# Moving two small VectorE operations: a lower limit to GpSimd, an affine step of the scan's decay to ScalarE

## The chip, the cores and the metric

The kernel runs on one core of a Trainium2 chip. Such a core has four engines that matter here: TensorE (PE in the profile; its weight loads are a row of their own, PEld), VectorE (DVE), ScalarE (ACT) and GpSimd (POOL). SyncE (SP) issues most of the transfers. Each engine takes its instructions in the order in which they stand in its own queue, and waits on semaphores for what other engines or transfers have to deliver. The metric is the device time of the whole kernel in microseconds (us). Before the change the median of three runs is 3594.73 us (3590.82 to 3597.36).

## The reference

The input x has 32 sequences of 256 tokens with 256 features. Two blocks follow each other, and x is added to their result.

```python
# block 1: a gated scan (d_inner 512, 16 states)
xr, gate = split(x @ W_in.T); xr = xr + t_emb
xc = silu(causal_conv4(xr) + b_conv)
xn = layernorm(xc) * ln_g + ln_b
Bm, Cm, dt = split(xn @ W_xproj.T, 3)
dt = tanh(dt @ W_dt.T + b_dt) * 0.01
Ad = 1.0 + dt * (-tanh(A_log))          # the decay factors
Bd = Bm * minimum(norm(xn), 1.0)
h  = clip(h * Ad + Bd * xt, -10, 10)    # 256 steps in order
y  = Cm . h + D * xn
out = (y * silu(gate)) @ W_out.T
# block 2, two layers (8 heads of 64, windows of 128 tokens)
q, k, v = split(shift(x) @ wqkv, 3)
q = q / clip(norm(q), 1e-12) * q_scale  # the same for k
q, k = rotary_xpos(q, k)
x = x + local_attention(q, k, v) @ wo
a, g = split(layernorm(shift(x)) @ w1 + b1)
x = x + (a * gelu(g)) @ w2 + b2
```

Two places matter: the decay factors `Ad`, and the lower limit that keeps the division of q and k by their lengths finite.

## The kernel before, in words

The 32 sequences are worked through in four groups of eight. The scan of a group runs in 8 chunks of 32 steps. All 128 lanes hold 16 states of 8 sequences; a step (line 716) is one VectorE instruction on a 128x512 tile that adds a row to the state and limits it. The kernel does not multiply the state by its decay. It carries the state divided by the running product `p` of the decays. For each chunk, `figures_in` (lines 627 to 639) makes the small tiles `bcd` and `beta`; `decay_th` (641 to 644) takes the hyperbolic tangent on ScalarE into `ad`, 128x32; `decays` (646 to 662) turns `ad` into decay factors on VectorE (648), multiplies them up with a scan instruction (650), takes the reciprocal (653), and from these makes `beta`, `ct` and the limits `lim`, the last on GpSimd (660, 661). Every step's row comes by a transfer from DRAM that repeats it over 16 states (`xrep`, 685, six buffers) and is scaled by its `beta` on ScalarE (706). TensorE reads the states out (728).

Block 2 works on one sequence at a time. `project_qkv` (984) multiplies for q, k and v and for two windows of 128 tokens. `rotated` (998 to 1023) handles one 128x512 tile of q or k, four per sequence and layer, 256 in all. ScalarE squares the tile (1002). VectorE makes the two rotary products (1005 and twice 1010) and sums the squares per head into `ss`, 128x8 (1015). VectorE then puts a lower limit on `ss` (1019). GpSimd adds the rotary products (1013), raises `ss` to the power -0.5 (1021) and scales the tile (1022). `turn` transposes the tile on TensorE (1028), and scores (1215), exponentials (1227), row sums (1252), their reciprocal on VectorE (1260), values (1271), output projection (1039) and the feed-forward part (1375 with gelu at 1386 and product at 1393, 1402) follow.

The order is set in two steps. The kernel's own code emits the work by slots: the scan's work hangs on step numbers, block 2's on eight slots per sequence, and the two are woven together, so that block 2 of one group runs beside the scan of the next. The framework's planner then orders the instructions of all engines by its own cost estimates, except where a line asks to keep the program's order. So a change of one instruction can move others in the queues. A chunk of the scan falls on two passes of a sequence through a layer. The first group's scan has nothing of block 2 beside it, and block 2 of the last group has no scan beside it.

All PSUM tiles come from one pool of eight banks. TensorE therefore also waits for VectorE or ScalarE to have read an older bank, whatever it was used for. The tiles `sq`, `swp` and the store tile `fo` share three buffers.

Of the kernel before, what the change touches and what calls it, by code (L numbers as in the profile page):

```python
# [13 lines left out]
AF = mybir.ActivationFunctionType  # L14
ALU = mybir.AluOpType
# [37 lines left out]
def bc(ap, axis, n):  # L53

    ap = ap.unsqueeze(axis)
    shape = list(ap.shape)
    shape[axis] = n
    return ap.broadcast_to(shape)
# [15 lines left out]
def kernel(  # L74
# [29 lines left out]
    nc = tc.nc  # L104
# [10 lines left out]
    def per_state(src, name):  # L115

        t = const.tile([P, 1], FP, tag=name, name=name)
        src = bc(bc(src, 1, GB), 2, 1)
        nc.scalar.dma_start(out=t, in_=src)
        return t  # L120
# [22 lines left out]
    a_sb = per_state(a_log, "a_sb")  # L143
# [24 lines left out]
    one = const.tile([P, 1], FP, tag="one", name="one")  # L168
# [53 lines left out]
    def program(ctx, exact):  # L222
# [154 lines left out]
        def group_scan(g):  # L377
# [263 lines left out]
            def decay_th(c):  # L641
                ad = sm.tile([P, CH], FP, tag="ad", name="ad")
                nc.scalar.activation(ad, ck[c]["bcd"][:, 2], AF.Tanh, bias=wbias[:, 2:3])
                ck[c]["ad"] = ad

            def decays(c):
                ad, bcd, beta = ck[c].pop("ad"), ck[c].pop("bcd"), ck[c]["beta"]
                nc.vector.tensor_scalar(ad, ad, a_sb, 1.0, ALU.mult, ALU.add)
                pd = sm.tile([P, CH], FP, tag="pd", name="pd")
                nc.vector.tensor_tensor_scan(pd, ad, zero_ch, state["p"], ALU.mult, ALU.add)  # L650
                state["p"] = pd[:, CH - 1 : CH]
                pi = sm.tile([P, CH], FP, tag="pi", name="pi")
                nc.vector.reciprocal(pi, pd)
                nc.vector.tensor_mul(beta, beta, pi)
                ct = sm.tile([P, CH], FP, tag="ct", name="ct")
                nc.vector.scalar_tensor_tensor(
                    ct, bcd[:, 1], wbias[:, 1:2], pd, ALU.add, ALU.mult
                )
                lim = sm.tile([P, 2, CH], FP, tag="lim", name="lim")
                nc.gpsimd.tensor_scalar_mul(lim[:, 0], pi, CLIP)  # L660
                nc.gpsimd.tensor_scalar_mul(lim[:, 1], pi, -CLIP)
                ck[c].update(ct=ct, lim=lim)
# [193 lines left out]
            for c in range(NCH):  # L856
# [28 lines left out]
                at(s0 - 9, figures, c)  # L885
                at(s0 - 7, figures_in, c)
                at(s0 - 6, decay_th, c)
                at(s0 - 5, decays, c)
                at(s0 - 4, put_c, c, 0)
                at(s0 + 4, put_c, c, 1)  # L890
# [107 lines left out]
        def rotated(l, ps, w, a):  # L998


            sq = ap_.tile([P, DI], FP, tag="swp", name="sq", bufs=3)
            nc.scalar.activation(sq, ps, AF.Square)  # L1002
            rot = ap_.tile([P, HEADS, DH], FP, tag="rot", name="rot", bufs=4)
            ph = ps.rearrange("p (h d) -> p h d", h=HEADS)
            nc.vector.tensor_mul(rot, ph, bc(rc_sb[:, l, w, a], 1, HEADS))  # L1005
            swp = ap_.tile([P, HEADS, DH], FP, tag="swp", name="swp", bufs=3)
            hd = DH // 2
            for i in range(2):
                o, s = slice(i * hd, (i + 1) * hd), slice((1 - i) * hd, (2 - i) * hd)
                nc.vector.tensor_mul(  # L1010
                    swp[:, :, o], ph[:, :, s], bc(rs_sb[:, l, w, a, o], 1, HEADS)
                )
            nc.gpsimd.tensor_add(rot, rot, swp)  # L1013
            ss = aw.tile([P, HEADS], FP, tag="ss", name="ss")
            nc.vector.tensor_reduce(
                ss, sq.rearrange("p (h d) -> p h d", h=HEADS), AX.X, ALU.add
            )

            nc.vector.tensor_scalar_max(ss, ss, 1e-24)  # L1019
            rn = aw.tile([P, HEADS], FP, tag="rn", name="rn")  # L1020
            nc.gpsimd.tensor_tensor(rn, ss, neg_half, ALU.pow)  # L1021
            nc.gpsimd.tensor_mul(rot, rot, bc(rn, 2, DH))  # L1022
            return rot
# [38 lines left out]
        def attention(l):  # L1062

            for b in range(GB):

                qTs, kTs, vs = [], [], []
                for w in range(NW):
                    for a in (2, 0, 1):
                        ps = project_qkv(b, w, a)
                        if a == 2:  # L1070
                            v_sb = ap_.tile([P, DI], FP, tag="v1", name="v_sb", bufs=3)
                            nc.scalar.copy(v_sb, ps)
                            vs.append(v_sb)
                            continue
                        rot = rotated(l, ps, w, a)
                        dst = ap_.tile(
                            [P, HEADS // 2, W], FP, tag="kT1" if a else "qT1",
                            name="kT" if a else "qT", bufs=3 if a else 2,
                        )
                        turn(rot, dst)  # L1080
                        (kTs if a else qTs).append(dst)
                        yield
# [71 lines left out]
        class Attention:  # L1154
# [9 lines left out]
            def project(self, b, w, a):  # L1164
                if w == 0 and a == 2:
                    self.qkv[b] = [
                        ap_.tile([P, HEADS // 2, S], FP, tag=n, name=n, bufs=1)
                        for n in ("qT", "kT")
                    ] + [ap_.tile([P, NW, DI], FP, tag="v", name="v_sb")]
                ps = project_qkv(b, w, a)  # L1170
                if a == 2:
                    nc.scalar.copy(self.qkv[b][2][:, w], ps)
                else:
                    self.rot[b, w, a] = rotated(self.l, ps, w, a)
# [487 lines left out]
```

## Time and profile before

| | |
|---|---|
| median of three runs | 3594.73 us |
| profiled execution, its own time | 3592.27 us |
| span of that profile, first to last instruction | 3590.5 us |
| TensorE busy | 3448.4 us, 96% |
| VectorE busy | 2667.8 us, 74% |
| ScalarE busy | 1979.5 us, 55% |
| GpSimd busy | 1874.5 us, 52% |
| line 1019, VectorE, x256 | 118.2 us, 462 ns each |
| line 648, VectorE, x32 | 22.0 us, 689 ns each |
| line 643, ScalarE, x32 | 10.2 us, 319 ns each |
| line 1021, GpSimd, x256 | 466.3 us, 1822 ns each |

A row of groups gives line, engine, operation, tiles and shapes, the number of instructions, their busy time and the mean of one, and then the idle time of the engine ahead of them with what ended it. Busy TensorE time is modelled from the instruction's size, so a stretch in which it is always busy is read together with the pitch of its instructions. The span falls into stages: up to about 475 us the first group's scan alone, to about 2700 us both blocks side by side, and then block 2 of the last group alone.

### The profile page before, as it was taken

How to read it: one execution, taken by the hardware profiler on the slowest of the kernel's cores; microseconds unless marked ns; L12 is line 12 of the kernel's file. 1: busy time of each engine (PE TensorE's matmuls, PEld its weight loads, DVE VectorE, ACT ScalarE, POOL GpSimd, SP SyncE). 2: the span in 40 equal slices, each digit the busy share in tenths (PEclk: the TensorE clock that was granted, in tenths of full speed). 3: DMA queues.
4: the chain of work that ended last, by engine and by line, in shares of the span. 5: the costliest groups of instructions: out<-in, count | busy, mean ns of one | idle time of the engine just before them, and what ended most of it. 6: DMA issues, size and time to landing. Idle time of an engine off the chain costs nothing.

```text
span 3590.5 us, 57544 instructions
## 1 busy us (share of the span) xinstructions
PE 3448.4 (96%) x20220; PEld 2253.8 (63%) x20220; DVE 2667.8 (74%) x5049; ACT 1979.5 (55%) x3535; POOL 1874.5 (52%) x1842
## 2 busy tenths in 40 slices
PE   7999989999999999999999999999999999999999
PEld 4545335566656666666666666666666677777777
DVE  5888989878788877877787888777777555555553
ACT  4656656656555655566566555665656444434442
POOL 4433467546556556655555566555545454544551
PEclk9999999999999999999999999999999999999999
DMA  7788755444444555444454555534353112011111
GB/s 201 215 209 220 201 156 151 131 112 139 129 134 127 147 146 142 138 117 125 118 140 127 135 149 139 146 107 130 113 143 118 56 49 64 13 30 36 34 27 37
DMA packets 468766, 435.67 MB, mean 121 GB/s; under 512 B 228723, under 2 KB 308084, under 8 KB 468340
## 3 DMA queue, kind: packets, MB, share of 16 engines
q1 hardware_dynamic: 384018, 419.88, 41.9%
q10 hardware_dynamic: 84450, 12.01, 2.0%
q8 instruction: 163, 2.67, 0.3%
q14 instruction: 135, 1.11, 0.1%
HBM read 383.54 MB, written 46.66 MB: 120 GB/s over the span
## 4 chain that ended last, share of the span: by engine, by line
PE 62%; DVE 19%; DMA 7%; POOL 5%; issue 3%; ACT 3%; SPq 1%; ACTq 0%; DVEq 0%; POOLq 0%
PE pa L1375 13%; PE ps_qkv L989 13%; DVE h L716 7%; PE po_f L1402 7%; PE ps_wo L1039 5%; DMA xrep<-xnd 5%; PE y L728 4%; PE ov L1271 3%; PE sc L1215 3%; PE ps_out L808 2%; PE ps_in L399 2%; PE tr_qk L1028 2%; PE rs L1252 2%; DVE acc L489 2%; PE ps_raw L518 1%
## 5 line engine op out<-in xcount | busy, mean ns | idle before, releaser
L716 DVE CUSTOM_DVE_ANT_0 h<-h,xrep,lim 128x512 f32<-128x512 f32 x1024 | 956.3, 934 | 195.5 <-ACT xrep L706 164.6
L706 ACT ACTIVATE xrep<-xrep,beta 128x512 f32<-128x512 f32 x960 | 673.6, 719 | 358.8 <-DMA xrep<-xnd 258.4
L989 PE MATMUL ps_qkv<-qkv,res 128*128 128x512 f32 x1536 | 713.5, 600 | 18.9 <-DVE rinv L1260 8.2
L1375 PE MATMUL pa<-hT,w 128*128 128x256 f32 (+1 forms) x2816 | 675.1, 382 | 11.8 <-DVE zT L799 11.4
L1375 PEld LDWEIGHTS pa<-hT,w 128*128 128x128 f32 (+1 forms) x2816 | 516.8, 188 | 153.6 <-issue 35.0
L1013 POOL TENSOR_TENSOR rot<-rot,swp 128x512 f32<-128x512 f32 x256 | 341.5, 1334 | 448.9 <-DVE swp L1010 399.5
L1021 POOL TENSOR_TENSOR rn<-ss,neg_half 128x8 f32<-128x8 f32 x256 | 466.3, 1822 | 16.7 <-DVE ss L1019 7.0
L989 PEld LDWEIGHTS ps_qkv<-qkv,res 128*128 128x128 f32 x1536 | 281.8, 191 | 302.3 <-issue 239.6
L728 PE MATMUL y<-h,ly 128*32 128x512 f32 x2048 | 347.2, 611 | 14.9 <-DVE h L716 13.9
L1327 POOL TENSOR_TENSOR rstd<-ve,neg_half 128x2 f32<-128x2 f32 x64 | 46.6, 727 | 524.6 <-DVE ve L1325 508.4
L1402 PE MATMUL po_f<-ag,w 128*128 128x256 f32 x1280 | 307.4, 387 | 6.9 <-DVE fo L1413 4.0
L1022 POOL TENSOR_TENSOR rot<-rot,rn 128x512 f32<-128x512 f32 x256 | 287.4, 1123 | 19.9
L1393 DVE SCALAR_TENSOR_TENSOR ag<-pa,b_sb,ag 128x256 f32<-128x256 f32 x320 | 151.6, 474 | 181.2 <-ACT ag L1386 181.0
L1402 PEld LDWEIGHTS po_f<-ag,w 128*128 128x128 f32 x1280 | 235.9, 191 | 72.0 <-issue 12.0
L1386 ACT ACTIVATE ag<-pa,b_sb 128x256 f32<-128x256 f32 x320 | 150.4, 470 | 232.6 <-PE pa L1375 231.5
L1002 ACT ACTIVATE sq<-ps_qkv 128x512 f32<-128x512 f32 x256 | 151.5, 596 | 199.8 <-PE ps_qkv L989 132.4
L489 DVE SCALAR_TENSOR_TENSOR acc<-xr,wc_sb,acc 128x256 f32<-128x256 f32 x384 | 196.9, 536 | 51.0 <-POOL acc L478 50.5
L1005 DVE TENSOR_TENSOR rot<-ps_qkv,rc_sb 128x512 f32<-128x512 f32 x256 | 174.9, 683 | 78.1 <-ACT sq L1002 77.7
L1039 PE MATMUL ps_wo<-oT,wo 128*128 128x256 f32 x1024 | 231.6, 379 | 0.0
L1039 PEld LDWEIGHTS ps_wo<-oT,wo 128*128 128x128 f32 x1024 | 194.5, 190 | 27.2 <-ACT sq L1002 0.8
L1227 ACT ACTIVATE pT<-sc 128x512 f32<-128x512 f32 x384 | 202.4, 603 | 7.8 <-PE sc L1215 6.0
L1271 PE MATMUL ov<-pT,v_sb 128*64 128x256 f32 (+1 forms) x2048 | 184.3, 330 | 19.3 <-DVE ag L1393 19.3
(159 smaller groups left out, 5462.8 us busy)
## 6 DMA issues: line engine op xcount, KB each, us to landing
xrep<-xnd SPq DMA_DIRECT2D x960, 256.0 KB
rb<-inv SPq DMA_DIRECT2D x128, 256.0 KB
xnd<-xn SPq DMA_DIRECT2D x64, 256.0 KB
qkv<-in_wqkv_dram SPq DMA_DIRECT2D x24, 512.0 KB
ahead<-xs_a SPq DMA_DIRECT2D x48, 256.0 KB
xp<-ahead SPq DMA_DIRECT2D x48, 256.0 KB
xd<-xnd SPq DMA_DIRECT2D x192, 64.0 KB
w<-in_w_dram SPq DMA_DIRECT2D x80, 128.0 KB
```

The lines of the kernel that those rows point to most:

```text
L489: nc.vector.scalar_tensor_tensor(acc, xr[:, :, k : k + CH], wc_sb[:, ch, k : k + 1], acc, ALU.mult, ALU.add,)
L706: scaled = nc.scalar.activation(bx, ck[c].pop(("bx", t), bx), AF.Copy, scale=ck[c]["beta"][:, t : t + 1])
L716: nc.vector._custom_dve(TENSOR_ADD_SAT, out=h_new, in0=state["h"], in1=bx, s0=ck[c]["lim"][:, 0, t : t + 1], s1=ck[c]["lim"][:, 1, t : t + 1],
L728: nc.tensor.matmul(ck[c]["y", hb][32 * q : 32 * q + 32, :], ly[hb % 2][:, 32 * t : 32 * t + 32], ck[c].pop(("h", hb * TB + t)), start=(i = ...
L989: nc.tensor.matmul(ps, res[b][:, k, t0 : t0 + W], wt["qkv", a][:, k], start=(k == 0), stop=(k == KM - 1),)
L1013: nc.gpsimd.tensor_add(rot, rot, swp)
L1021: nc.gpsimd.tensor_tensor(rn, ss, neg_half, ALU.pow)
L1022: nc.gpsimd.tensor_mul(rot, rot, bc(rn, 2, DH))
L1039: nc.tensor.matmul(po[:, d], wt["wo", 0][:, c, d * P : (d + 1) * P], oT[:, c, :], start=(c == 0), stop=(c == NC_ - 1),)
L1271: nc.tensor.matmul(ov[r * DH : (r + 1) * DH, i, kw * W :], self.qkv[b][2][:, kw, h * DH : (h + 1) * DH], self.p.pop((b, kw, i0 + i, r)), s ...
L1375: nc.tensor.matmul(dst[x], wt["w1", m][:, k, x], self.h[:, k], start=(k == 0), stop=(k == KM - 1),)
L1402: nc.tensor.matmul(self.po[:, d], wt["w2", 0][:, m, d * P : (d + 1) * P], self.ag[m], start=(m == 0), stop=(m == len(MCH) - 1),)
```

## The change

The lower limit on `ss` is issued on GpSimd, directly ahead of the power that reads it. The affine step that makes `ad` a decay factor, 1 + a*tanh, is issued on ScalarE as a second activation (`Identity`, with the constant 1 as bias and `a_sb` as scale, both one value per lane) directly behind the tangent, and no longer on VectorE. Nothing else is edited. Lines after 648 keep their numbers; the new activation is line 644, and 643 stays the tangent.

```diff
             def decay_th(c):
                 ad = sm.tile([P, CH], FP, tag="ad", name="ad")
                 nc.scalar.activation(ad, ck[c]["bcd"][:, 2], AF.Tanh, bias=wbias[:, 2:3])
+                nc.scalar.activation(ad, ad, AF.Identity, bias=one, scale=a_sb)
                 ck[c]["ad"] = ad
 
             def decays(c):
                 ad, bcd, beta = ck[c].pop("ad"), ck[c].pop("bcd"), ck[c]["beta"]
-                nc.vector.tensor_scalar(ad, ad, a_sb, 1.0, ALU.mult, ALU.add)
                 pd = sm.tile([P, CH], FP, tag="pd", name="pd")
@@ rotated @@
-            nc.vector.tensor_scalar_max(ss, ss, 1e-24)
+            nc.gpsimd.tensor_scalar_max(ss, ss, 1e-24)
             rn = aw.tile([P, HEADS], FP, tag="rn", name="rn")
             nc.gpsimd.tensor_tensor(rn, ss, neg_half, ALU.pow)
```

## The prediction

> **What bounds the kernel now.** First the busy time by stages. The columns are the stretch, its length, then busy time and number of instructions of PE, PEld, DVE, ACT and POOL, granted clock, DMA share and GB/s.
>
> ```profile
> 0.00:475.00 475.00, 425.37 (x1776) 219.03 (x1776) 386.49 (x709) 278.13 (x500) 189.94 (x289) 0.96 0.77 209
> 475.00:720.00 245.00, 224.25 (x1290) 127.61 (x1290) 218.77 (x400) 145.02 (x264) 158.14 (x153) 0.97 0.50 140
> 720.00:1314.00 594.00, 567.09 (x3480) 371.84 (x3480) 487.15 (x906) 351.40 (x634) 331.83 (x323) 0.99 0.49 134
> 1314.00:2700.00 1386.00, 1349.18 (x8392) 896.39 (x8391) 1095.67 (x2105) 824.95 (x1489) 789.89 (x742) 1.00 0.48 131
> 2700.00:3590.50 890.50, 882.54 (x5287) 638.96 (x5285) 479.70 (x934) 380.02 (x651) 404.66 (x338) 1.00 0.17 46
> ```
>
> TensorE's idle time is length less busy time: 49.6, 20.8, 26.9, 36.8 and 8.0 us, 142 in all. The last stage is nothing but TensorE: its chain of work is made of TensorE lines alone (`pa` 25.5%, `ps_qkv` 23.6%, `po_f` 14.6%), and the 8 us lie at the very end. What is won before 2700 us arrives whole at the end; in the last stage nothing is won. From 1314 us the same pattern of two sequences and one chunk of the scan repeats 13 times, in 101.4 to 103.7 us, mean 102.5. So I ask what TensorE waits for there (total us, times, longest):
>
> ```profile
> PE ov L1271 <- DVE ag L1393: 16.4, 12, 1.4
> PE ps_qkv L989 <- DVE rinv L1260: 7.9, 12, 0.9
> PE pa L1375 <- DVE zT L799: 7.8, 6, 2.0
> PE ps_qkv L989 <- DVE xd L779: 3.1, 11, 0.6
> PE ps_qkv L989 <- DVE ag L1393: 0.5, 1, 0.5
> ```
>
> These 35.7 us are nearly all of the 36.8, and each is VectorE being late, though it is busy only 79% here. Why it is late is in the instructions of one pattern, in order of time (start, length, engine, line); first VectorE, then GpSimd, then TensorE:
>
> ```profile
> 1575.25 0.81 DVE L716 CUSTOM_DVE_ANT_0 h<-h,xrep,lim 128x512 f32<-128x512 f32 x1
> 1575.97 1.02 DVE L1019 TENSOR_SCALAR ss<-ss 128x8 f32<-128x8 f32 x1
> 1576.90 0.68 DVE L799 TENSOR_TENSOR zT<-tz,sg 128x512 f32<-128x512 f32 x1
> ...
> 1579.69 0.80 DVE L716 CUSTOM_DVE_ANT_0 h<-h,xrep,lim 128x512 f32<-128x512 f32 x1
> 1580.41 1.02 DVE L648 TENSOR_SCALAR ad<-ad,a_sb 128x32 f32<-128x32 f32 x1
> 1581.34 1.82 DVE L716 CUSTOM_DVE_ANT_0 h<-h,xrep,lim 128x512 f32<-128x512 f32 x1
> 1583.09 0.27 DVE L650 TENSOR_TENSOR_SCAN pd<-ad,pd,zero_ch 128x32 f32<-128x32 f32 x1
> 1583.28 0.45 DVE L1393 SCALAR_TENSOR_TENSOR ag<-pa,b_sb,ag 128x256 f32<-128x256 f32 x1
> ```
>
> ```profile
> 1575.78 1.18 POOL L1022 TENSOR_TENSOR rot<-rot,rn 128x512 f32<-128x512 f32 x1
> 1580.32 1.06 POOL L1022 TENSOR_TENSOR rot<-rot,rn 128x512 f32<-128x512 f32 x1
> 1581.35 1.26 POOL L758 TENSOR_TENSOR xd<-xd,dskip_sb 128x512 f32<-128x512 f32 x1
> ```
>
> ```profile
> 1583.88 0.87 PE L1271 MATMUL ov<-pT,v_sb 128*64 128x256 f32 x8 [1.36 <-DVE ag L1393]
> ```
>
> Lines 1019 and 648, tiny, take 1.02 us each, and end just as GpSimd's L1022 ends. Both stand ahead of the `ag` for which TensorE then idles 1.36 us.
>
> [...] 1019 takes 151 ns at best, 462 in the mean, 1076 at most. [...] lines 579 and 1353, `Identity` too, have no load of their own.
>
> **The change part by part.**
>
> Removed from VectorE: 118.2 us (256 x 462 ns) and 22.0 us (32 x 689 ns), 140 of 2668.
>
> Added to GpSimd: 256 limits on 128x8, not in the trace. Nearest row: L660, 128x32 with one tensor input, 0.38 us from its start to that of its twin L661 (1584.68 to 1585.06). Line 478, 128x256, takes 0.80 against L660's 0.31, so 24 columns fewer save 0.05: I take 0.33 us, 84 us in all. Bounds: 0.10 (the smallest GpSimd instruction, a memset) and 0.62 (L661 beside VectorE), 26 to 159 us. GpSimd goes from 52% to 55%. Queued behind are the power, the scaling 1022 and `tr_qk`. TensorE waits for 1022 three times in the kernel, 6.1 us, all between 475 and 720; in the pattern above, 1022 ends at 1581.4 and its transpose runs at 1588.6, 7 us later, which covers 2 x 0.33. Without that cover it would cost up to 0.66 a pair, 128 pairs, 84 us.
>
> Added to ScalarE: 32 activations with two pointers. [...] ScalarE has that time: from 1314 on it idles in front of 643 for VectorE 14 times, 53.2 us. Lower bound 0.23 (the start-to-start pitch behind 643)[...].
>
> Moved by the planner: in the repeating pattern TensorE, ScalarE, GpSimd and SP keep their orders apart from the additions. On VectorE one place changes: `pd` (650), which stood behind an `h`, takes the place of 648, and `pi`, `ct`, `beta` and `res` go ahead of the next `ag`. That is 1.08 us more in front of `ag` (starts from 1583.65 to 1584.73). DMA numbers don't change; the order of a few transfers does in the first 1300 us.
>
> *1314 to 2700 us.* Without the two 1019s VectorE reaches `zT` about 1.0 to 1.3 us earlier (pitch 0.07 to 0.37, and 0.93), and the place of 648 the same. `pd` finds its input: [...] beta, an `ag` and an `h`, over 1.4 us, stand between. `h` then runs in 0.8 us, since L758 comes later, instead of 1.82. So `ag` starts at about 1583.28 - 1.2 - 0.93 - 1.0 + 1.08 = 1581.2, and TensorE wants it at 1582.5: the 16.4 us go, less 1 or 2. `rinv` ends 0.7 us too late and everything ahead of it (the buffer that `h` frees, its transfer, the scaling, gelu) comes over 1.5 us earlier: 6 of 7.9. `zT`: about 1 of 1.3 us each, 5 of 7.8; in half of the patterns the delay comes from a store transfer that stays. `xd`: 2.5 of 3.1. Sum 28.5. A pattern without waits would be about 2.5 us shorter than now, 33 over the stage; I take 30.
>
> *720 to 1314.* VectorE loses 25.9 + 3.8 us of 487. TensorE's 26.9 idle us are scattered over sixteen causes, some on ScalarE. A third: 8.
>
> *475 to 720.* VectorE is 89% busy; 14.6 + 1.9 us go. Five VectorE lines alone hold 30% of the chain there, so a good third of it: 6; but `rn` holds 4.4% of that chain, 10.8 us or six powers, each now with a limit ahead of it: 2 back. 4.
>
> *0 to 475.* No 1019. 648 takes 0.24 us, and VectorE waits for the tangent six times, 10.9 us, all here[...] nothing, -1.
>
> *From 2700.* 23.9 us of VectorE go, behind TensorE without a gap: 0.
>
> Sum 30 + 8 + 4 - 1 = 41 us. Against the profiled execution, 3592.3, that gives 3551.3; the median of the runs lies 2.4 higher, so 3553.7. I say 3553.
>
> **The rivals.** *A wait takes the place*: TensorE comes earlier and the next late thing shows, the row's transfer and its scaling (ScalarE waited for `xrep` 88.2 us in the repeating stage) or the regrouped `ag`. For: `ag`'s margin is 1.3 us on a sum of five terms. Half of it: 18 to 20 us, 3575. *Hidden anyway*: TensorE is 96% busy, the waits are short and the planner's new order in the first 1300 us costs what is won: 3592. Against: 42 of 42 waits in the repeating stage name VectorE. *Slower*: [...] VectorE waits for it instead. `h` [...] takes 705 ns at best, 934 in the mean[...]. It decides from 140/256 = 0.55 us per limit, under L661's worst, 0.64; at 0.62 VectorE is 19 us worse off and the pairs of transposes come 1.2 us later where they are tight: 3605. *More*: all of the middle's 84 us of idle time can't go; two thirds give 3535.
>
> **How the numbers follow.** Forecast 0.63 (its own range 3536 to 3570), half 0.18, hidden 0.08, slower 0.05, more 0.06. Holding 8 in 10: leaving out the lower part of "more" and what lies above half: 3532 to 3586. A measurement of this kernel can tell about 0.2%, 7 us, from no change. Faster: 0.63 + 0.18 + 0.06, same 0.08, slower 0.05.
>
> **What would show it.** Waits of TensorE for `ag`, `rinv`, `zT` and `xd` under 12 us from 35.7; the repeating pattern at about 100 us; line 1019 on GpSimd near 0.33 us start to start; 643 and 644 together under 0.7 us; the last stage as long as before, 890 us. Wrong would be: `ov` still idle for `ag`, 1019 on GpSimd over 0.55, `pd` waiting for the identity in the middle stage, or `tr_qk` waiting for 1022 often.

## The result, and where the time went

The changed kernel is slower: 3614.66 us against 3596.05, medians of six runs each; the ratio is 1.0044 (95% interval 1.003 to 1.0057), some 16 us. One of the changed kernel's six runs was in a slow state of the chip (3665.86 us, at a granted clock of 0.942) and stays out of the ratio; the median of the other five is 3613.51. The forecast was 3553. The two profiled executions lie a little further apart, 3592.3 and 3616.0.

First the last four of the stretches shown before; the columns are again the stretch, its length, busy time and instructions of PE, PEld, DVE, ACT and POOL, granted clock, DMA share and GB/s.

```profile
475.00:720.00 245.00, 217.02 (x1256) 123.50 (x1256) 204.22 (x365) 145.14 (x266) 166.97 (x174) 0.94 0.51 141
720.00:1314.00 594.00, 574.19 (x3482) 375.49 (x3481) 466.67 (x858) 354.16 (x641) 341.83 (x365) 0.98 0.49 134
1314.00:2700.00 1386.00, 1340.93 (x8295) 882.43 (x8293) 1047.90 (x1962) 817.43 (x1483) 819.86 (x842) 1.00 0.47 129
2700.00:3614.30 914.30, 906.52 (x5418) 655.68 (x5418) 482.11 (x885) 395.46 (x678) 445.02 (x432) 1.00 0.17 48
```

From 1314 to 2700 us VectorE did get lighter (1047.90 us busy against 1095.67) and GpSimd heavier (819.86 against 789.89). TensorE is idle there for 45.1 us, not 36.8. The stretches are cut at fixed times, so the delay itself is read from the starts of the scan's chunks (first step of each, line 716), after minus before: +3.6 us at 443, +8.9 at 792, +6.4 at 1284, and from there steadily up to +24.0 at 2710. It stays there to the end (+23.8): the last stage is as long as it was. Most of the loss, 17.6 us, is in the repeating pattern, which now takes 103.8 us in the mean instead of 102.5. The 6.4 us ahead of it are less sure: these are single executions, and the granted clock was lower in this one from 475 to 1314 us (0.94 and 0.98 against 0.97 and 0.99). In the repeating stage it was 1.00 in both.

What TensorE waits for from 1314 to 2700 us (total us, times, longest):

```profile
PE ps_qkv L989 <- DVE rinv L1260: 9.2, 11, 0.9
PE ps_qkv L989 <- DVE ag L1393: 8.1, 10, 0.9
PE pa L1375 <- DVE zT L799: 7.2, 9, 1.5
PE ov L1271 <- ACT xn L579: 5.9, 13, 0.7
PE tr_qk L1028 <- DVE ag L1393: 4.2, 5, 1.3
PE ps_qkv L989 <- DVE xd L779: 3.2, 12, 0.5
```

The 16.4 us of `ov` behind `ag` are down to 0.5. In their place stand waits of `ps_qkv` and `tr_qk` for a later `ag`, and one that was not in the list before: `ov` waits for `xn`, 13 times, once per pattern.

Two new delays can be seen in one pattern. The first is on ScalarE. Before, in order of time (start, length, engine, line; in brackets the idle time ahead and what ended it):

```profile
1579.77 0.57 ACT L1033 COPY qT<-tr_qk 128x512 f32<-128x512 f32 x1
...
1584.90 0.72 ACT L706 ACTIVATE xrep<-xrep,beta 128x512 f32<-128x512 f32 x1 [3.46 <-DVE beta L654]
```

and after, the same place:

```profile
1593.86 0.72 ACT L706 ACTIVATE xrep<-xrep,beta 128x512 f32<-128x512 f32 x1 [4.29 <-DMA xrep<-xnd]
1594.49 0.56 ACT L1033 COPY qT<-tr_qk 128x512 f32<-128x512 f32 x1
1594.95 0.59 ACT L1033 COPY kT<-tr_qk 128x512 f32<-128x512 f32 x1
1595.43 1.34 ACT L706 ACTIVATE xrep<-xrep,beta 128x512 f32<-128x512 f32 x2
```

The scaling of the new chunk's first row, which waited for `beta` behind the copies of `qT` and `kT`, now stands ahead of them. In the repeating stage this is the only change in ScalarE's order apart from the addition, and it is there in all 13 patterns. `beta` is ready at 1591.2 (line 654), but the row lands only at about 1593.8, and the copies, whose transposes (1028) had ended at 1586.90, the old chunk's last rows and a gelu queue behind it. VectorE and TensorE show what that makes late:

```profile
1596.20 1.66 DVE L716 CUSTOM_DVE_ANT_0 h<-h,xrep,lim 128x512 f32<-128x512 f32 x2 [4.00 <-ACT xrep L706]
1597.77 0.48 DVE L1393 SCALAR_TENSOR_TENSOR ag<-pa,b_sb,ag 128x256 f32<-128x256 f32 x1
```

```profile
1590.48 2.90 PE L1271 MATMUL ov<-pT,v_sb 128*64 128x256 f32 x32
...
1598.40 0.63 PE L1028 MATMUL tr_qk<-ident,rot 128*128 128x128 f32 x4 [1.22 <-DVE ag L1393]
```

`ov` is unbroken now; what VectorE had won there it loses a little later, when `h` waits 4.00 us for a row that is scaled behind the copies (1595.43). The profile page's rows of these groups (the idle time of the engine ahead of them is the last part) say the same for the whole kernel: `h` waited 164.6 us for the scaling before, and the scaling 258.4 us for rows.

```profile
L716 DVE CUSTOM_DVE_ANT_0 h<-h,xrep,lim 128x512 f32<-128x512 f32 x1024 | 954.6, 932 | 243.0 <-ACT xrep L706 210.0
L706 ACT ACTIVATE xrep<-xrep,beta 128x512 f32<-128x512 f32 x960 | 674.4, 719 | 357.3 <-DMA xrep<-xnd 309.4
```

The second delay is GpSimd's. The chain of work that ended last runs over GpSimd for 12% of the span; before it was 5%. Which of the two costs what, the traces of two kernels can't say.

### The profile page after: what moved, and what is told of

It reads as the page before. It is cut to its first block, busy times and chain, and to the rows that moved or that the text cites. A ratio compares the mean times of both kernels' runs of the same rounds, so it can differ in the third digit from the quotient of the medians.

```text
span 3614.3 us, 57526 instructions
## 1 busy us (share of the span) xinstructions
PE 3467.9 (96%) x20220; PEld 2255.3 (62%) x20220; DVE 2581.4 (71%) x4761; ACT 1991.8 (55%) x3567; POOL 1966.2 (54%) x2098
## 4 chain that ended last, share of the span: by engine, by line
PE 58%; DVE 15%; POOL 12%; DMA 9%; ACT 4%; issue 3%; SPq 0%; ACTq 0%; POOLq 0%; DVEq 0%
PE ps_qkv L989 13%; PE pa L1375 12%; DMA xrep<-xnd 7%; PE po_f L1402 7%; DVE h L716 6%; PE y L728 4%; PE ov L1271 3%; PE ps_wo L1039 3%; PE sc L1215 3%; POOL rot L1013 3%; POOL rn L1021 3%; PE ps_in L399 2%; DVE acc L489 2%; PE ps_out L808 2%; PE tr_qk L1028 2%
## 5 line engine op out<-in xcount | busy, mean ns | idle before, releaser
L989 PE MATMUL ps_qkv<-qkv,res 128*128 128x512 f32 x1536 | 723.0, 606 | 29.4 <-DVE rinv L1260 9.4
L1013 POOL TENSOR_TENSOR rot<-rot,swp 128x512 f32<-128x512 f32 x256 | 364.9, 1426 | 446.7 <-DVE swp L1010 398.3
L1021 POOL TENSOR_TENSOR rn<-ss,neg_half 128x8 f32<-128x8 f32 x256 | 447.6, 1748 | 21.3
L1022 POOL TENSOR_TENSOR rot<-rot,rn 128x512 f32<-128x512 f32 x256 | 274.8, 1073 | 20.0
L1010 DVE TENSOR_TENSOR swp<-ps_qkv,rs_sb 128x256 f32<-128x256 f32 x512 | 191.6, 415 | 31.2 <-POOL rot L1013 30.9
```

The lines of the kernel that those rows point to most:

```text
L989: nc.tensor.matmul(ps, res[b][:, k, t0 : t0 + W], wt["qkv", a][:, k], start=(k == 0), stop=(k == KM - 1),)
```

## The experiments

Each ratio is to the kernel before in runs on the same chip, with its 95% interval.

**The two halves.** Theory A: GpSimd's longer row costs. Theory B: the planner's new order costs. The limit alone on GpSimd:

```diff
-            nc.vector.tensor_scalar_max(ss, ss, 1e-24)
+            nc.gpsimd.tensor_scalar_max(ss, ss, 1e-24)
```

> Half of the change: the lower limit on GpSimd, the decay factors on VectorE as before. Theory A (GpSimd: the limit lengthens GpSimd's row of rotary sum, limit, power and scaling[...]): this half carries the loss, 3608 to 3618 us. Theory B (order: the planner's new places for the scan's decay steps and row loads make ScalarE meet a row's transfer that has not landed, with gelu and the copies of qT and kT queued behind it): this half does not lose, 3570 to 3596 us, and ScalarE's waits for rows stay near the 258 us of before.

Measured: 3597.61 us, ratio 0.9994 (0.9987 to 1.0002). The decay step alone on ScalarE:

```diff
+                nc.scalar.activation(ad, ad, AF.Identity, bias=one, scale=a_sb)
...
-                nc.vector.tensor_scalar(ad, ad, a_sb, 1.0, ALU.mult, ALU.add)
```

> The other half: the decay factors completed on ScalarE, the lower limit on VectorE as before. Theory A (GpSimd): 3588 to 3597 us, a gain of at most a few us. Theory B (order): this half carries the loss, 3605 us or more, with ScalarE's waits for rows at about 300 us, as in the changed kernel.

Measured: 3600.25, ratio 0.9994 (0.9986 to 1.0002). Neither half alone costs or wins anything that these runs can tell; the loss comes only with both, so neither theory in its simple form holds. Two more kernels take the limit out, once with the decay step on VectorE, once on ScalarE.

```diff
-            nc.vector.tensor_scalar_max(ss, ss, 1e-24)
```

> The kernel before with no lower limit at all: that part of the computation is left out, on both engines. Its order differs from that of the kernel with the limit alone on GpSimd in nothing but the limit's own instructions (nearly so), so the difference of the two is the price of the limit on GpSimd. Theory A: 20 us or more below that kernel, 3570 to 3590. Theory B: within 8 us of it.

Measured: 3566.97, ratio 0.9906 (0.9891 to 0.9920).

> The changed kernel without any lower limit: that part of the computation is left out. Theory A: well below the kernel before, 3565 to 3590 us, since GpSimd has nothing added. Theory B: still above the kernel before, 3600 to 3612 us.

Measured: 3581.93, ratio 0.9946 (0.9932 to 0.9960).

Together these four and the changed kernel make a full table, in per cent of the kernel before:

| limit | decay on VectorE | decay on ScalarE |
|---|---|---|
| on VectorE | 0 | -0.06 |
| none | -0.94 | -0.54 |
| on GpSimd | -0.06 | +0.44 |

Taking the limit off VectorE wins 0.94%, 34 us. Putting it on GpSimd costs 0.88%, 32 us. The decay step on ScalarE does nothing while the limit is on VectorE, and costs 0.40 to 0.50%, 14 to 18 us, as soon as it isn't. So A and B are both at work: -34 + 32 + 18 = +16 us. (These are three steps of one path through the table, so that their sum has to come out.) The step of 32 us is a clean one: from 1284 us on, the kernels without a limit and with it on GpSimd have the same order on TensorE, VectorE, ScalarE and GpSimd, the limit apart.

**Why the decay step costs: the order on ScalarE.** In the kernels where it costs, the first row's scaling stands ahead of the copies, as shown above; in the one where it costs nothing (limit on VectorE) it stands behind them, as before, in 12 of the 13 patterns, although the Identity and the earlier `pd` are there too. The kernels without a limit show it with GpSimd left out of the matter. Without the decay step on ScalarE:

```profile
2071.66 0.57 ACT L1033 COPY qT<-tr_qk 128x512 f32<-128x512 f32 x1
...
2075.54 0.72 ACT L706 ACTIVATE xrep<-xrep,beta 128x512 f32<-128x512 f32 x1 [2.20 <-DVE beta L654]
```

and with it, in the same pattern:

```profile
2089.83 0.72 ACT L706 ACTIVATE xrep<-xrep,beta 128x512 f32<-128x512 f32 x1 [3.19 <-DMA xrep<-xnd]
2090.45 0.57 ACT L1033 COPY qT<-tr_qk 128x512 f32<-128x512 f32 x1
```

Measured from the chunk's first step, in the mean over 13 patterns, the `qT` copy starts at 87.66 us in the first and 91.56 in the second; the pattern takes 100.66 and 101.83 us. To test it, the first row of a chunk is requested one step later in the changed kernel, which puts the copies ahead again:

```diff
-                    at(s0 + t - 2, scale_row, c, t)
+                    at(s0 + t - (1 if t == 0 and not alone else 2), scale_row, c, t)
```

> The changed kernel with the scaling of the first row of a chunk asked for one step later (not in the first group), so that the planner puts the copies of qT and kT ahead of it on ScalarE. Theory B (order: the loss of the ScalarE part comes from the copies and gelu standing behind a row that has not landed): 3592 to 3602 us, as with the limit alone. If instead the Identity itself or the earlier pd costs: 3610 us or more, as the changed kernel.

Measured: 3595.17, ratio 0.9970 (0.9954 to 0.9987). From 1.0044, 0.74% are gone with one request; the Identity and the earlier `pd` are still there, so they are not what cost. But 0.74% is more than the 0.50% that the decay step had cost, and the edit does more than put the old order back: in each pattern one scaling of a row stands 9 places further back on ScalarE than in the kernel before, and one step `h` 8 places further back on VectorE. A kernel with the later request and the limit alone on GpSimd was not run, so what the copies' place is worth by itself stays open. The same edit in the kernel before, as a control:

> Control: the same later request for a chunk's first row in the kernel before. There the copies already stand ahead of that scaling. Theory B: within 5 us of the kernel before. A gain of 10 us or more would say that the later request helps whatever the change does.

Measured: 3600.34, ratio 0.9992 (0.9984 to 1.0000): next to nothing. And with the decay step on ScalarE and the limit on VectorE:

> The ScalarE half of the change with the later request for a chunk's first row, the limit on VectorE as before. Theory B (order): the decay step is worth a few us once the copies are not behind the row: 3585 to 3596 us. If the decay step on ScalarE is worth nothing in itself: within 5 us of the kernel before.

Measured: 3600.53, ratio 0.9996 (0.9985 to 1.0006). The decay step on ScalarE is worth nothing even in this order.

The later request seems to have a price of its own. In their profiles the three kernels with it come to the chunk that began at 1284 us 13 to 17 us later than the same kernels without it. In the repeating pattern they are quicker: 101.7 us instead of 103.8 in the changed kernel, 102.3 instead of 102.5 in the kernel before. Single profiles can differ by some us ahead of that chunk, so this is an indication and not a measured price.

**Why the limit on GpSimd costs: what stands behind it.** One place in a pattern, first in the kernel without a limit:

```profile
2313.52 1.28 POOL L1013 TENSOR_TENSOR rot<-rot,swp 128x512 f32<-128x512 f32 x1
2314.76 1.64 POOL L1021 TENSOR_TENSOR rn<-ss,neg_half 128x8 f32<-128x8 f32 x1
...
2324.03 0.55 POOL L565 TENSOR_TENSOR stat<-ve,neg_half 128x1 f32<-128x1 f32 x1
```

and then with the limit alone on GpSimd:

```profile
2341.80 1.29 POOL L1013 TENSOR_TENSOR rot<-rot,swp 128x512 f32<-128x512 f32 x1
2343.04 0.25 POOL L1019 TENSOR_SCALAR ss<-ss 128x8 f32<-128x8 f32 x1
2343.38 2.16 POOL L1021 TENSOR_TENSOR rn<-ss,neg_half 128x8 f32<-128x8 f32 x1
...
2348.30 0.68 POOL L1019 TENSOR_SCALAR ss<-ss 128x8 f32<-128x8 f32 x1
...
2353.04 0.55 POOL L565 TENSOR_TENSOR stat<-ve,neg_half 128x1 f32<-128x1 f32 x1
```

From the first rotary sum to `stat` it takes 10.51 us without limits and 11.24 with two. GpSimd has no idle time here. `stat` (565) leads by way of VectorE (571) and ScalarE (579) to `xn`, and this kernel shows the wait that was new in the changed one, while the kernel without a limit has none:

```profile
PE ov L1271 <- ACT xn L579: 6.5, 13, 0.9
```

Is it the tile's own chain (theory C) or the queue behind the pair (theory D)? The limit is moved behind the scaling of its tile, where it has no effect; from 1284 us on, every other instruction keeps its order (edit against the kernel with the limit alone on GpSimd):

```diff
-            nc.gpsimd.tensor_scalar_max(ss, ss, 1e-24)
             rn = aw.tile([P, HEADS], FP, tag="rn", name="rn")
             nc.gpsimd.tensor_tensor(rn, ss, neg_half, ALU.pow)
             nc.gpsimd.tensor_mul(rot, rot, bc(rn, 2, DH))
+            nc.gpsimd.tensor_scalar_max(ss, ss, 1e-24)
```

> The kernel with the limit on GpSimd alone, but the limit stands behind the scaling of its tile (line 1022), not ahead of its power, so that nothing of the tile waits for it: the power takes the unlimited sum, which leaves the lower limit without effect. All other instructions keep the order of that kernel on every engine. Theory C (own chain: the limit costs because power, scaling and transpose of its own tile come later): close to the kernel without any limit, 3566 to 3576 us. Theory D (queue: it costs because the scan's preparation and the masks that stand behind the pair on GpSimd come later by two limits): as with the limit in its place, 3593 to 3602 us.

Measured: 3581.02, ratio 0.9949 (0.9932 to 0.9966), half way between the two, in neither range. The mean times in the pattern, from the chunk's first step, explain a part:

| | `stat` 565, second | `xn` 579, second | `stat` 600 | pattern |
|---|---|---|---|---|
| no limit | 37.23 | 38.01 | 64.99 | 100.66 us |
| limit behind its tile | 37.65 | 38.46 | 66.44 | 101.58 us |
| limit ahead of its power | 38.14 | 38.92 | 66.39 | 102.61 us |

What stands behind the pair comes later even when no power waits for the limit, and this kernel loses about 0.43%, 15 us: the queue costs without the tile's own chain (D). In its real place the limit delays `stat` 565 and `xn` by twice as much (0.91 against 0.42 and 0.45 us), `stat` 600 by the same, and the pattern grows by 1.95 instead of 0.92 us. TensorE has no wait for 1022, where the tile's own chain ends, in this stage in any of the three, and the traces speak against C for the other 16 us too. TensorE waits 34.2 us in this stage with the limit in its place and 21.2 with it behind its tile; half of the difference, 6.5 us, is `ov` waiting for `xn`, which hangs on `stat` 565.

A rival that these runs do not rule out is VectorE waiting for GpSimd's limits. In the changed kernel's trace 274 of the 1024 steps `h` take over 850 ns, and 269 of these end 0.52 to 0.56 us after the end of a GpSimd instruction, as if they waited for it; how often that is a limit is not shown. VectorE's busy time, with the same instructions in all three kernels, is 2574.6 us without a limit, 2579.2 with the limit behind its tile and 2600.3 with it in its place. If VectorE's time is worth as much here as when the limit left it (34 us for 93 us less of it), that is some 2 us of the first 15 and 8 of the other 16, an estimate. How the 16 us divide is not shown.

The third engine was tried for the limit too; there it is an addition of 1e-24, `tiny` being a column of that value:

```diff
-            nc.vector.tensor_scalar_max(ss, ss, 1e-24)
+            nc.scalar.activation(ss, ss, AF.Identity, bias=tiny)
```

> The lower limit on the third engine: ScalarE adds 1e-24 to the sum (Identity with a bias) in the place of VectorE's maximum; the decay as before. Theory D (GpSimd's queue is what the limit costs there, VectorE's what it costs before): most of the 35 us of the kernel without a limit are kept, 3568 to 3585 us, unless the added wait of GpSimd's power for ScalarE, which itself waits for rows, takes it back: then 3590 us or more.

Measured: 3593.87, ratio 0.9973 (0.9962 to 0.9984). The waits of ScalarE in the repeating stage say why (lines are one higher in this kernel): it now waits in its queue for VectorE's sums, and for rows half as long again as the 88.2 us of before.

```profile
ACT xrep L707 <- DMA xrep<-xnd: 133.8, 47, 5.5
...
ACT ss L1020 <- DVE ss L1016: 82.6, 56, 5.3
```

**What VectorE's price for the limit is.** The limit can stay on VectorE in a form that does not wait: the sums go into the first column of pairs whose second column holds 1e-24, and a reduction takes the maximum of each pair; two such tiles take turns. From 1284 us on, every engine's order is that of the kernel before.

```diff
+    pair = [const.tile([P, HEADS, 2], FP, tag=f"pair{i}", name=f"pair{i}") for i in range(2)]
+    [nc.gpsimd.memset(t, 1e-24) for t in pair]
...
+            pr = pair[turn_of[0] % 2]; turn_of[0] += 1
...
-                ss, sq.rearrange("p (h d) -> p h d", h=HEADS), AX.X, ALU.add
-            )
+                pr[:, :, 0], sq.rearrange("p (h d) -> p h d", h=HEADS), AX.X, ALU.add)
...
-            nc.vector.tensor_scalar_max(ss, ss, 1e-24)
+            nc.vector.tensor_reduce(ss, pr, AX.X, ALU.max)
```

> The kernel before with its limit still on VectorE, in another form: the sums go into the first column of pairs whose second column holds 1e-24 from the start, and a maximum over each pair is taken by the same instruction type as line 1015 (a reduction, which never took over 680 ns, while the limit took up to 1076). Every engine keeps the order of the kernel before. Theory F (most of VectorE's price for the limit is waiting for GpSimd [...]): the limit is short every time, near 0.17 us, and about two thirds of the 35 us come without moving anything, 3570 to 3582 us. If its mere place and work on VectorE costs: within 8 us of the kernel before.

Measured: 3568.37, ratio 0.9913 (0.9895 to 0.9932), nearly all of what leaving the limit out gives. Line 1019 before, and as a reduction (min/median/max in ns, first and last start, forms):

```profile
L1019 DVE TENSOR_SCALAR ss<-ss x256: 151/336/1076, 483.5 to 3500.7; 128x8 f32<-128x8 f32 x128
```

```profile
L1019 DVE TENSOR_REDUCE ss<-pair x256: 148/159/170, 484.4 to 3470.3; 128x8 f32<-128x16 f32 x128
```

At its quickest the old form took the same 0.15 us; what cost was the waiting. 178 of its 256 took over 200 ns, 593 in the mean or 105 of the line's 118 us, and every one of these ended 25 to 35 ns after the end of a GpSimd instruction; the other 78 took 163 ns in the mean. Last, this reduction together with the decay step on ScalarE and the later first row:

> Both cures together: the limit as a reduction on VectorE, the decay completed on ScalarE, the first row of a chunk requested one step later. Theories B and F add: 3562 to 3578 us, faster than both kernels by 0.7% or more. If the row transfers then take over: no better than the reduction alone.

Measured: 3567.74, ratio 0.9911 (0.9888 to 0.9934): no better than the reduction alone. Its profile shows a quicker pattern, 100.05 us against 100.56, but it comes to the chunk at 1284 us 16 us later than the reduction's. Both versions beat the kernel before and the changed one, by 0.9% and 1.3%; the reduction alone is the smaller edit.

## Why the prediction was wrong

*What bounds the kernel* held. So did the worth of VectorE's time: the forecast's 41 us for 140 us of VectorE stands against 34 us for the limit's 118 when it is left out, and 31 when it no longer waits. All of it came from the limit. The decay step, 22 us of VectorE, was worth nothing (0.9994, and 0.9996 with the later request); the prediction lumped it with the limit and did not size it alone.

*Added to GpSimd* is the first step that failed, by its cover and not mainly by its price. The cover named the power, the scaling and `tr_qk`, and found 7 us of slack there. That slack was real: TensorE waits for 1022 three times in the changed kernel, 6.6 us (6.1 before), none of them in the repeating stage. But it left out the other work queued on GpSimd behind the pair, `stat` (565, 600), the masks (1238) and `acc` (478), on which VectorE, ScalarE and then TensorE depend: with the limit alone on GpSimd `stat` 565 comes 0.91 us later in the pattern than without one, and `ov` waits for `xn` in each of the 13. The price was under-sized too: the median from the limit's start to the next instruction's is 0.33 us, as forecast, but the mean is 0.47, 121 us in all and not 84. The step "up to 0.66 a pair without cover, 84 us" was there, and the forecast put it at nothing in the repeating stage; it came to 32 us, some of which may be VectorE waiting for GpSimd.

*Moved by the planner* is the second. The prediction said that ScalarE keeps its order apart from the additions. It does not: the scaling of a new chunk's first row passes the two copies. The decay step, which brings that about, costs 14 to 18 us, and a later request for that row takes more than this away. The move on VectorE that was named (`pd` forward, 1.08 us ahead of `ag`) did no harm by itself: `ov` no longer waits for `ag`, 0.5 us of 16.4.

*By stages*: for the stretch to 475 us -1 was forecast, on an estimate of the identity's length (it took 397 to 416 ns, line 644), and the changed kernel lost 3.6; from there to about 800, where some gain was forecast, it lost 5 more; to 1284 it got 2.5 back of the 8 forecast; in the repeating stage it lost 17.6 where 30 were to be won; in the last stage nothing changed, as forecast. Part of what was lost from 475 us on may be the lower clock. VectorE also waits for the identity there, twice and 6.1 us in all, which the forecast did not have; the kernel without a limit waits 5.6 us there for the tangent itself, so it is not the identity's own length.

*The rivals*: "a wait takes the place" named the right wait, the row's transfer and its scaling, but took it for half of the gain. By the table it took 18 of 34 us, and the limit on GpSimd 32. "Slower" had the right sign with a mechanism that carries a part of it at most: it decided from 0.55 us per limit by VectorE waiting for GpSimd, but the mean was 0.47 and VectorE did get lighter, by 86 us (2667.8 to 2581.4), if not by 140. Some of the difference may be such waiting: from 1314 to 2700 us a step `h` takes 908 ns in the mean without a limit and 951 with it alone on GpSimd, some 19 us over that stage's 431 to 441 steps. In "more", two thirds of 84 us would give 3538 and not 3535; nothing hangs on it.

*The signs*: the waits for `ag`, `rinv`, `zT` and `xd` came to 33.9 us, not under 12; the pattern to 103.8 us, not 100. From the start of 643 to the start of what follows 644 it took 0.67 us, `pd` never waited for the identity in the repeating stage, and the last stage kept its length, all as foreseen. The changed kernel has 126 table loads on ScalarE (`ACT_TABLE_LOAD`, 1283 ns each), as many as before.

## What to carry to other kernels

A small instruction moved to an engine that is 52% busy isn't free (32 us here): list everything that stands behind it in that engine's queue, not only what reads its result, and follow each to the engine that sets the end. After a small edit elsewhere a planner may put an instruction further forward than its slowest input, here a transfer (why it did so here was not tested); compare the order of every engine around each wait, ScalarE's too. If a tiny operation is mostly waiting, as 105 of the limit's 118 us suggest here, look first for a form of it that doesn't wait (the reduction, never over 170 ns), and only then for another engine.

## What the runs showed of the hardware

A reduction of 128x16 to 128x8 on VectorE took 148 to 170 ns in all 256 cases, in the very place where the maximum with a constant took 151 to 1076. Line 1015, a reduction too, took 664 to 680 ns in all 256 cases in the kernel before. In the same trace 277 of the 1024 steps `h` took over 850 ns (705 at best), and 273 of these ended 0.52 to 0.56 us after the end of a GpSimd instruction; the long cases of the maximum ended just behind one too, as shown above. The same limit on GpSimd took 230 to 751 ns in the changed kernel. With the limit alone on GpSimd, moving it behind its tile shortened the rotary sums (1013) from 1429 to 1291 ns in the mean and lengthened the limit from 389 to 469 ns. How long GpSimd's own instructions take changes with their place; why was not shown.
